# Moving a router's choice into the middle of a block product, and the next adjacency one gap later, in a fused graph-attention and expert kernel

## The chip, the cores and the metric

The kernel runs on one core of one Trainium2 chip. A core has five engines that matter here, each with an instruction queue of its own: TensorE (PE in the profile, its weight loads PEld), VectorE (DVE), ScalarE (ACT), GpSimd (POOL) and SyncE (SP), which only starts transfers. They meet through semaphores. The metric is the device time of one execution in microseconds (us), as the median of several runs.

## The reference

There are 128 graphs of 128 nodes with 1024 features, and a 0/1 adjacency for each graph. First a graph attention with 16 heads of 64 features is added, then a mixture of two out of eight low-rank experts. Cut to what matters:

```python
def gnn(h, adj, W, a):                       # h = layernorm(x)
    Wh = h @ W                               # 128 x 1024 for each graph
    e = leaky_relu(Wh1 + Wh2)                # both per node and head: Wh . a
    att = softmax(where(adj == 0, NEG_INF, e), axis=-1) * adj
    return elu(att @ Wh)

x = x + gnn(layernorm(x), adj, W, a)

y = layernorm(x)
logits = y[:, 0, :] @ router_w.T             # first node of a graph, 8 experts
gates = softmax(top-2 of logits, the rest -inf)
x = x + y + sum over the two experts e: gate_e * (y @ down_e.T) @ up_e.T     # rank 16
```

## The kernel before

The graphs are taken in pairs, q = 0 to 63, and for the experts in groups of four, g = 0 to 31. For one pair `project` multiplies the 256 rows by W in a scheme of seven block products (a Strassen-Winograd form) in place of eight. Each product is eight matmuls of 260 columns in float32; the trace has two matmul records for each. The products of a pair accumulate in three PSUM tiles, "x", "y" and "z", that share a pool of two buffers, taken in turn:

```python
ps_w = ctx.enter_context(tc.tile_pool(name="ps_w", bufs=2, space=bass.MemoryType.PSUM))
# ...
def product(dst, first, lhs, rhs, half_way=None):
    order = [(j, k) for j in range(2) for k in range(KH)]     # KH = 4
    # ... (another order for q == 0)
    for at, (j, k) in enumerate(order):
        if half_way and at == KH:
            half_way()
        nc.tensor.matmul(dst[:, j, cols], lhs[:, k, :], w_sb[:, rhs, k, j, cols],
                         start=(first and k == 0), stop=(k == KH - 1),
                         skip_group_check=not first)
# ...
def read(dst, src, plus):
    nc.vector.tensor_tensor(dst[:, :, cols], src[:, :, cols], plus[:, :, cols], ALU.add)
# ... product_1 (x), product_6 (y), product_2 (x), product_5 (y)
def product_7():
    product(*to("z"), s3, T3, None if q else keep("", column_means, "part 1")[0])
    if q:
        read(wh[:, 2], banks["z"], u4)

def product_3():
    product(*to("y"), s4, B22)
    read(wh[:, 0], banks["y"], p1)

def product_4():
    product(*to("z"), a22, NT4, None if q else keep("scores", first_scores)[0])
    read(wh[:, 1], banks["z"], u2)

for step in ((product_1, product_6, product_2, product_5, product_7, product_3, product_4)
             if q else ...):
    step()
    yield
```

Product 3 is the sixth in order. Everything else of the pairs before and after stands in eight gaps, lists of calls that are carried out ahead of the products: what is in `gaps[6]` is issued between product 3 and product 4, `gaps[0]` ahead of product 1. The engines work through their own instructions in the order in which these calls issue them.

```python
for gap in gaps:
    for f, *args in gap:
        f(*args)
    next(products, None)
```

`pair_sums` (gap 4) makes the sums of input blocks for the next pair on GpSimd, four operations on 128x512. `row_parts` (gap 4) multiplies the first rows with the router, and `logits`, `choose` and `fetch` find the two experts of each of the four graphs and fetch their weights from a table in HBM:

```python
def row_parts(g):
    # ... prod = router_sb * row, part = sum of prod, on VectorE
    nc.vector.tensor_tensor(st["add"][:, 0:G * E].rearrange("p (g e) -> p g e", g=G),
                            of_graph[:, :, None].to_broadcast([P, G, E]),
                            part[:, None].to_broadcast([P, G, E]), ALU.mult)

def logits(g):
    st["pl"] = ps_m.tile([P, HALF], F32, tag="pm", name="pl")
    nc.tensor.matmul(st["pl"][:, 0:G * E + G], ones, st["add"], start=True, stop=True)

def choose(g):
    nc.vector.tensor_copy(lg, st["pl"][:, 0:G * E]...)
    for s in range(TOP):                                # TOP = 2
        if s:
            nc.vector.tensor_tensor(mark, by_order, val[:, 0, :, 0:1]..., ALU.is_equal)
            nc.vector.scalar_tensor_tensor(lg, mark, NO_ENTRY, lg, op0=ALU.mult, op1=ALU.add)
        nc.vector.tensor_reduce(top[:, s], lg, AX.X, ALU.max)
        nc.vector.tensor_tensor(mark, lg, top[:, s, :, None]..., ALU.is_equal)
        nc.vector.tensor_tensor(mark, mark, by_order, ALU.mult)
        nc.vector.tensor_reduce(val[:, 0, :, s], mark, AX.X, ALU.max)
    nc.vector.tensor_tensor(pr[:, 0], top[:, 1], top[:, 0], ALU.subtract)
    nc.vector.tensor_tensor(pr[:, 0], pr[:, 0], st["dev"], ALU.mult)

def fetch(g):
    # ... four small operations on VectorE make the row numbers at_down and at_up
    for j in range(G * TOP):
        nc.gpsimd.indirect_dma_start(out=st["down"]..., in_=table, in_offset=...at_down[:, j:j + 1])
    nc.gpsimd.indirect_dma_start(out=st["up"], in_=up_t, in_offset=...at_up[:, 0:1])
```

`group_adj` counts the entries of each row of the four adjacencies and makes the value that a masked entry is given; `load_adj` loads the adjacencies of the next group, into `adj_i` (one buffer, SyncE's queue) and `adj_f` (two buffers, GpSimd's queue). The attention of a group first uses `n` and `neg` in gap 0 of the following pair.

```python
def group_adj(g):
    nc.vector.tensor_scalar(nz, st["adj_i"], 0.0, None, op0=ALU.not_equal)
    nc.vector.tensor_reduce(n[:, 0], nz, AX.X, ALU.add)
    nc.gpsimd.tensor_scalar(n[:, 1], n[:, 0], -1.0, float(N), op0=ALU.mult, op1=ALU.add)
    nc.gpsimd.tensor_scalar(full, n[:, 1], 0.0, NO_ENTRY, op0=ALU.is_equal, op1=ALU.mult)
    nc.gpsimd.tensor_scalar(neg, full, NEG_INF, None, op0=ALU.min)
```

`high` (ScalarE, gaps 6 and 7) and `low` (VectorE) split a block of the result into two parts for the attention's matmuls, `attend` (gaps 1 and 2). `ffn_down` and `ffn_up` apply the fetched experts during the odd pair that follows.

Of the kernel before, what the change touches and what calls it, by code (L numbers as in the profile page):

```python
# [14 lines left out]
ALU = mybir.AluOpType  # L15
AX = mybir.AxisListType

NEG_INF = -9000000000000000.0
NO_ENTRY = -3.0e38
# [6 lines left out]
def adj_ffn_kernel(  # L26
# [16 lines left out]
    nc = tc.nc  # L43
    B, N, D = x.shape
# [14 lines left out]
    NG, _, G, _ = adj.shape  # L59
# [28 lines left out]
    B11, B21, B22, T1, T2, T3, NT4 = range(7)  # L88
# [317 lines left out]
    def group_adj(g):  # L406

        st = GRP[g]
        nz = work.tile([P, G, N], F32, tag="hp", name="nz")
        nc.vector.tensor_scalar(nz, st["adj_i"], 0.0, None, op0=ALU.not_equal)  # L410

        n = small.tile([P, 2, G], F32, tag="n", name="n")
        nc.vector.tensor_reduce(n[:, 0], nz, AX.X, ALU.add)
        nc.gpsimd.tensor_scalar(n[:, 1], n[:, 0], -1.0, float(N), op0=ALU.mult, op1=ALU.add)

        full = small.tile([P, G], F32, tag="full", name="full")
        nc.gpsimd.tensor_scalar(full, n[:, 1], 0.0, NO_ENTRY, op0=ALU.is_equal, op1=ALU.mult)
        neg = small.tile([P, G], F32, tag="negv", name="negv")
        nc.gpsimd.tensor_scalar(neg, full, NEG_INF, None, op0=ALU.min)
        st.update(n=n, neg=neg)  # L420

    def project(q):

        xt = XT.pop(q)
        a11, a12, a22 = xt[:, 0, 0:KH], xt[:, 0, KH:KC], xt[:, 1, KH:KC]
        s1, s2, s3, s4 = SUMS.pop(q)

        wh = WH[q] = work.tile([P, 3, 2, QE], F32, tag="wh", name="wh", bufs=1)
        if q:
            SC[q] = small.tile([P, 2, HPQ], F32, tag="sc", name="sc")
        PARTS[q] = work.tile([P, 2, 2 * NH, HALF], F32R, tag="parts", name="parts", bufs=1)


        cols = slice(0, QE) if q else MAIN

        def bank():
            return ps_w.tile([P, 2, HALF], F32, tag="pw", name="pw")  # L440

        def product(dst, first, lhs, rhs, half_way=None):
            order = [(j, k) for j in range(2) for k in range(KH)]
            if q == 0:
                order.sort(key=lambda at: at[1])
# [7 lines that stand above are left out]
        def temp(tag):  # L453
            return work.tile([P, 2, QE], F32, tag=tag, name=tag, bufs=1)

        def read(dst, src, plus):
            nc.vector.tensor_tensor(dst[:, :, cols], src[:, :, cols], plus[:, :, cols], ALU.add)  # L457

        p1, u2, u4 = (temp(n) for n in ("p1", "u2", "u4"))
        WH["p1"] = p1  # L460
        banks = {}

        def to(name):
            if name not in banks:
                banks[name] = bank()
                return banks[name], True
            return banks[name], False

        def product_1():
            product(*to("x"), a11, B11)  # L470
            nc.scalar.copy(p1[:, :, cols], banks["x"][:, :, cols])

        def product_2():
            product(*to("x"), a12, B21, None if q else keep("", column_means, "part 0")[0])
            WH[q, 0] = banks["x"]
            if q:
                high(q, 0)
                nc.scalar.copy(SC[q], banks["x"][:, :, SCORES])

        def product_6():  # L480
            product(*to("y"), s2, T2)
            read(u2, banks["y"], p1)

        def product_5():
            product(*to("y"), s1, T1)
            read(u4, banks["y"], p1)
            if q == 0:
# [5 lines that stand above are left out]
                read(wh[:, 2], banks["z"], u4)  # L493

        def product_3():
            product(*to("y"), s4, B22)
            read(wh[:, 0], banks["y"], p1)

        def product_4():
# [5 lines that stand above are left out]
                     if q else  # L505
                     (product_1, product_2, product_7, product_6, product_5, product_3, product_4)):
            step()
            yield
# [7 lines left out]
    def high(q, b):  # L516
        block, rstd = of_block(q, b)
        nc.scalar.mul(in_two(PARTS[q][:, 0, b]), block, rstd)  # L518
# [383 lines left out]
    def correct(less, halves):  # L902
        c, by = (WH[0, 0], less[:, 2:3]) if halves == 2 else (WH["p1"][:, :, MAIN], less[:, 0:1])
        nc.vector.scalar_tensor_tensor(c, w_mean[0], by, c, op0=ALU.mult, op1=ALU.add)

    got = {}

    def keep(name, f, *of):

        def task():  # L910
            got[name] = f(*(got.get(o, o) for o in of))
        return (task,)
# [23 lines left out]
    for q in range(NQ + 2):  # L936
        gaps = [[] for _ in range(8)]
        if q == 0:
            prepare(gaps)
        g, part = divmod(q - 2, 2)  # L940
        ffn = 0 <= g < NG
        if ffn and not part:
            gaps[6] += [(logits, g), (choose, g)]
            if g < NG - 1:
                gaps[6].append((fetch, g))
        if q < NQ:
            gaps[6] += [(high, q, 3), (high, q, 1)]
            gaps[7].append((high, q, 2))
# [49 lines left out]
            gaps[5].insert(0, (ffn_up, (g, 0)))  # L998
            gaps[6].append((ffn_up, (g, 1)))
        if q % 2 == 0 and q < NQ:  # L1000
            gaps[5].append((group_adj, q // 2))
            if q // 2 + 1 < NG:
                gaps[5].append((load_adj, q // 2 + 1))
        if q < NQ:
            if q:
                gaps[3].insert(0, (low, q, 0))
# [62 lines left out]
```

## Time and profile before

| what | value |
|---|---|
| median of 3 runs | 1895.14 us (1893.79 to 1895.28) |
| span of the profiled execution | 1893.3 us |
| TensorE busy | 1880.4 us, 99% |
| VectorE busy | 1714.6 us, 91% |
| ScalarE busy | 1085.0 us, 57% |
| GpSimd busy | 836.6 us, 44% |
| granted TensorE clock | 0.999 |

Busy time is the sum of an engine's executions, and a wait is the time in which it had none, put down to what released it. In a timeline line the first number is the start in us, the second the duration, then engine, line of the kernel, operation, tiles written and read, and in brackets the idle time ahead. Line 449 is the block products, 457 `read`, 727 the router's matmul, 694 the end of `row_parts`, 740 to 757 `choose`, 787 to 790 `fetch` on VectorE, 794 its transfers, 399 to 403 the pair sums, 410 and 413 `group_adj`, 522 `low`, 518 `high`.

### The profile page before, as it was taken

The numbers are of one execution on the slowest core, as the hardware profiler recorded it, in microseconds if no ns is written. First come the engines' busy times: TensorE is split into PE (matmuls) and PEld (weight loads), VectorE is DVE, ScalarE is ACT, GpSimd is POOL, SyncE is SP. The second block draws the span as 40 slices with busy tenths as digits, with TensorE's granted clock in tenths as the row PEclk, the third lists the DMA queues.
The fourth block names the chain that finished last, engine by engine and source line by source line (L and its number), as shares of the span: only waits on it lengthen the run. The fifth ranks groups of instructions, "written<-read, shape, count | busy, mean of one in ns | idle before, by whom it ended". The sixth has DMA issues, their size and how long they took to land.

```text
span 1893.3 us, 29564 instructions
## 1 busy us (share of the span) xinstructions
PE 1880.4 (99%) x10430; PEld 1553.0 (82%) x10430; DVE 1714.6 (91%) x3643; ACT 1085.0 (57%) x1063; POOL 836.6 (44%) x1173
## 2 busy tenths in 40 slices
PE   9999999999999999999999999999999999999997
PEld 6888888888888888888888888888888888888885
DVE  6899999999999999999999999999999999999997
ACT  3656556556556555565565565565655655655654
POOL 4345443355343355433553433554434544335530
PEclk9999999999999999999999999999999999999999
DMA  8465655655655656556556556565566566565544
GB/s 316 135 194 151 181 179 156 194 183 138 201 177 159 199 155 171 179 158 194 184 135 201 178 160 198 156 168 181 166 189 189 133 194 183 156 195 166 159 154 115
DMA packets 349100, 330.43 MB, mean 175 GB/s; under 512 B 279196, under 2 KB 281372, under 8 KB 348440
## 3 DMA queue, kind: packets, MB, share of 16 engines
q1 hardware_dynamic: 326760, 286.06, 50.6%
q0 software_dynamic: 17008, 40.91, 7.8%
q10 hardware_dynamic: 5184, 1.57, 0.3%
q8 instruction: 83, 1.36, 0.3%
q14 instruction: 65, 0.53, 0.1%
HBM read 194.24 MB, written 68.17 MB: 139 GB/s over the span
## 4 chain that ended last, share of the span: by engine, by line
PE 97%; DVE 2%; issue 1%; POOL 0%; DMA 0%; DVEq 0%; ACT 0%
PE pw L449 82%; PE ph L566 6%; PE pu L824 4%; PE pd L808 3%; POOL down L794 0%; PE pu L884 0%; PE idle L160 0%; DVE stats L346 0%; DMA down<-table,at_down 0%; PE pl L727 0%; DVE parts L522 0%; PE rows L238 0%; PE pd_all L859 0%; PE pc L209 0%; DVE xn L828 0%
## 5 line engine op out<-in xcount | busy, mean ns | idle before, releaser
L449 PE MATMUL pw<-w_sb,xt 128*128 128x260 f32 (+1 forms) x4080 | 936.3, 385 | 0.1
L449 PEld LDWEIGHTS pw<-w_sb,xt 128*128 128x128 f32 x4080 | 767.7, 190 | 146.0 <-issue 30.9
L449 PE MATMUL pw<-w_sb,s 128*128 128x260 f32 (+1 forms) x3072 | 707.9, 383 | 0.0
L449 PEld LDWEIGHTS pw<-w_sb,s 128*128 128x128 f32 x3072 | 580.7, 190 | 115.2 <-issue 12.6
L350 POOL TENSOR_SCALAR rstd<-mv 128x2 f32<-128x2 f32 x126 | 27.3, 217 | 847.4 <-DVE mv L347 842.1
L641 ACT COPY y_t<-tt 128x2048 uint16<-128x2048 uint16 x126 | 316.2, 2509 | 111.9 <-DMA tt<-halves 111.6
L635 ACT COPY halves<-xn 128x2048 uint16<-128x2048 uint16 x126 | 239.3, 1899 | 144.4 <-DVE xn L586 101.3
L346 DVE BATCH_NORM_STATS2 stats<-xn 128x6 f32<-128x512 f32 x500 | 316.3, 674 | 0.0
L794 POOL DMA_INDIRECT down<-table,at_down x248 | 259.3, 1045 | 91.1 <-issue 65.2
L583 ACT ACTIVATE ex<-hp 128x1024 f32<-128x1024 f32 x128 | 135.4, 1058 | 229.6 <-DVE hp L576 173.0
L518 ACT ACTIVATE parts<-wh,rstd 128x512 fp32r<-128x512 f32 x192 | 130.9, 714 | 197.7 <-DVE wh L457 197.7
L828 DVE SCALAR_TENSOR_TENSOR xn<-pu,rstd,xn 128x512 f32<-128x512 f32 x248 | 169.1, 745 | 19.9 <-PE pu L824 19.5
L576 DVE TENSOR_TENSOR hp<-ph,att 128x512 f32<-128x512 f32 x256 | 161.2, 671 | 10.1 <-PE ph L566 9.8
L586 DVE SCALAR_TENSOR_TENSOR xn<-ex,xn 128x1024 f32<-128x1024 f32 x126 | 154.4, 1225 | 13.6 <-issue 0.5
L566 PE MATMUL ph<-parts,adj_f 128*128 128x512 f32 x512 | 164.8, 443 | 1.3 <-ACT parts L518 0.8
L584 DVE SCALAR_TENSOR_TENSOR xn<-hp,xn 128x1024 f32<-128x1024 f32 x128 | 156.8, 1225 | 4.4
L661 ACT ACTIVATE xn<-xn,off,mul 128x1024 f32<-128x1024 f32 x128 | 151.3, 1231 | 0.0
L522 DVE SCALAR_TENSOR_TENSOR parts<-wh,rstd,parts 128x512 fp32r<-128x512 f32 x192 | 137.7, 745 | 1.6 <-ACT parts L518 1.5
L566 PEld LDWEIGHTS ph<-parts,adj_f 128*128 128x128 f32 x512 | 96.6, 189 | 21.1 <-ACT parts L518 1.2
L457 DVE TENSOR_TENSOR wh<-pw,u 128x520 f32<-128x520 f32 (+1 forms) x128 | 88.0, 688 | 10.7 <-PE pw L449 10.4
L351 POOL TENSOR_TENSOR rstd<-rstd,half_pow 128x2 f32<-128x2 f32 x126 | 90.2, 716 | 10.5
L457 DVE TENSOR_TENSOR u<-pw,p 128x520 f32<-128x520 f32 (+1 forms) x128 | 86.0, 672 | 6.9 <-remote 3.9
(175 smaller groups left out, 1456.4 us busy)
## 6 DMA issues: line engine op xcount, KB each, us to landing
xn<-in_x SPq DMA_DIRECT2D x128, 512.0 KB
xt<-in_x_t SPq DMA_DIRECT2D x127, 512.0 KB
out_y<-xn SPq DMA_DIRECT2D x124, 512.0 KB
adj_f<-in_adj_t POOLq DMA_DIRECT2D x32, 256.0 KB
adj_i<-in_adj SPq DMA_DIRECT2D x32, 256.0 KB
down<-table,at_down POOLq DMA_INDIRECT x248
w_sb<-in_w SPq DMA_DIRECT2D x3, 1040.0 KB
wt_sb<-in_w_t SPq DMA_DIRECT2D x1, 2048.0 KB
```

The lines of the kernel that those rows point to most:

```text
L346: nc.vector.bn_stats(st[:, h, :], X[i][:, h * HALF:(h + 1) * HALF])
L449: nc.tensor.matmul(dst[:, j, cols], lhs[:, k, :], w_sb[:, rhs, k, j, cols], start=(first and k == 0), stop=(k == KH - 1), skip_group_check ...
L457: nc.vector.tensor_tensor(dst[:, :, cols], src[:, :, cols], plus[:, :, cols], ALU.add)
L566: nc.tensor.matmul(PH[i][h], GRP[g]["adj_f"][:, t, :], PARTS[q][:, s, NH * (i % 2) + h], start=(s == 0), stop=(s == 1))
L576: nc.vector.tensor_tensor(hp[:, h * HALF:(h + 1) * HALF].rearrange("p (h f) -> p h f", f=F), ph.rearrange("p (h f) -> p h f", f=F), att[:, ...
L584: nc.vector.scalar_tensor_tensor(xt, hp, 0.0, xt, op0=ALU.max, op1=ALU.add)
L586: nc.vector.scalar_tensor_tensor(xt, ex, 1.0, xt, op0=ALU.min, op1=ALU.add)
L635: nc.scalar.copy(halves, X[i].bitcast(U16).rearrange("p (d s) -> p s d", s=2))
L641: nc.scalar.copy(y_of(i).bitcast(U16).rearrange("p k (n s) -> p s k n", s=2), TT.pop(i).rearrange("p (s k) n -> p s k n", s=2))
L661: nc.scalar.activation(X[i], X[i], AF.Identity, bias=GRP[g]["off"][:, t:t + 1], scale=GRP[g]["mul"][:, t:t + 1])
L794: nc.gpsimd.indirect_dma_start(out=st["down"][:, j * R:(j + 1) * R].rearrange("p r k -> p (r k)"), out_offset=None, in_=table, in_offset=b ...
L828: nc.vector.scalar_tensor_tensor(y[:, cols], pu[t], st["rstd"][:, t:t + 1], y[:, cols], op0=ALU.mult, op1=ALU.add)
```

## The change

For all groups but the last, logits, choice and fetch are no longer called in gap 6 of the even pair, behind product 3, but from within product 3, after four of its eight matmuls. On VectorE the choice so comes ahead of the `read` of product 3. Reading the adjacency and loading the next one move from gap 5 to gap 6, and the three small operations of `group_adj` move from GpSimd to VectorE, so that they do not stand in GpSimd's queue behind the nine transfers of the fetch. The fetch is meant to start earlier.

```diff
-        nc.gpsimd.tensor_scalar(n[:, 1], n[:, 0], -1.0, float(N), op0=ALU.mult, op1=ALU.add)
+        nc.vector.tensor_scalar(n[:, 1], n[:, 0], -1.0, float(N), op0=ALU.mult, op1=ALU.add)
...
-        nc.gpsimd.tensor_scalar(full, n[:, 1], 0.0, NO_ENTRY, op0=ALU.is_equal, op1=ALU.mult)
+        nc.vector.tensor_scalar(full, n[:, 1], 0.0, NO_ENTRY, op0=ALU.is_equal, op1=ALU.mult)
...
-        nc.gpsimd.tensor_scalar(neg, full, NEG_INF, None, op0=ALU.min)
+        nc.vector.tensor_scalar(neg, full, NEG_INF, None, op0=ALU.min)
...
         def product_3():
-            product(*to("y"), s4, B22)
+            product(*to("y"), s4, B22, between.get(q))
             read(wh[:, 0], banks["y"], p1)
...
+    between = {}
...
         if ffn and not part:
-            gaps[6] += [(logits, g), (choose, g)]
-            if g < NG - 1:
-                gaps[6].append((fetch, g))
+            if g == NG - 1:
+                gaps[6] += [(logits, g), (choose, g)]
+            else:
+                between[q] = lambda g=g: [f(g) for f in (logits, choose, fetch)]
...
         if q % 2 == 0 and q < NQ:
-            gaps[5].append((group_adj, q // 2))
+            gaps[6].append((group_adj, q // 2))
             if q // 2 + 1 < NG:
-                gaps[5].append((load_adj, q // 2 + 1))
+                gaps[6].append((load_adj, q // 2 + 1))
```

## The prediction

> **What bounds the kernel now.** I read the page first, then the waits of TensorE, then the timeline of one period. From the page, the busy row and the chain's shares by engine:
>
> ```profile
> PE 1880.4 (99%) x10430; PEld 1553.0 (82%) x10430; DVE 1714.6 (91%) x3643; ACT 1085.0 (57%) x1063; POOL 836.6 (44%) x1173
> PE 97%; DVE 2%; issue 1%; POOL 0%; DMA 0%; DVEq 0%; ACT 0%
> ```
>
> TensorE is busy for 99% of the span and carries 97% of the chain that ended last. Busy time of TensorE is modelled, so I checked it against starts. In the timeline below, the 16 matmul records of the sixth product begin at 668.52 and the router's matmul at 672.02: 3.50 us for 16, 0.219 us each, and that spacing holds through the products. The waits of TensorE hold only a handful of entries below 2.5 us each; away from the start and the end there is one in the whole run:
>
> ```profile
> PE pt L650 <- DVE xn L589: 2.4, 1, 2.4
> ...
> PE pd L808 <- DMA down<-table,at_down: 0.5, 1, 0.5
> ```
>
> The second, at 750 us, delays the next products by 0.95 us in all (58.64 us from one group's logits to the next, against 57.69 in all others). That one event is all that a better fetch can win. So in the steady part, 31 groups of 57.69 us, there is hardly anything to remove, and the question is whether the change brings in a wait.
>
> Here is the stretch the change touches, from the timeline at 668 to 677 us (start, duration, engine, line, operation):
>
> ```profile
> 668.52 3.67 PE L449 MATMUL pw<-w_sb,s 128*128 128x260 f32 x16
> ...
> 668.80 1.34 POOL L400 TENSOR_TENSOR s<-s,xt 128x512 f32<-128x512 f32 x1
> ...
> 669.49 0.69 DVE L694 TENSOR_TENSOR add<-of_graph,part 128x32 f32<-128x32 f32 x1
> 670.10 1.29 POOL L402 TENSOR_TENSOR xt<-xt 128x512 f32<-128x512 f32 x1
> 670.11 0.69 DVE L457 TENSOR_TENSOR wh<-pw,u 128x520 f32<-128x520 f32 x1
> 670.72 0.95 DVE L410 TENSOR_SCALAR nz<-adj_i 128x512 f32<-128x512 int32 x1
> 671.34 1.47 POOL L403 TENSOR_TENSOR s<-xt,s 128x512 f32<-128x512 f32 x1
> ...
> 672.02 0.31 PE L727 MATMUL pl<-add,ones 128*128 128x36 f32 x2
> ...
> 672.30 0.69 DVE L457 TENSOR_TENSOR wh<-pw,p 128x520 f32<-128x520 f32 x1
> ...
> 672.91 0.18 DVE L740 COPY lg<-pl 128x32 f32<-128x32 f32 x1
> ...
> 673.35 0.19 DVE L752 TENSOR_TENSOR mark<-lg,top 128x32 f32<-128x32 f32 x1
> 673.57 0.19 DVE L753 TENSOR_TENSOR mark<-mark,order 128x32 f32<-128x32 f32 x1
> ...
> 676.36 0.21 DVE L790 TENSOR_SCALAR at_up<-of_slot,up_row 128x1 uint32<-128x1 f32 x1
> ```
>
> VectorE works without a pause here, in the order of the program. The reader should see two things: the second read of `wh` (672.30, block product 3) is what frees the PSUM bank of that product, and today it stands ahead of the choice; and the four pair sums of GpSimd end at 672.81, just before the choice begins.
>
> **What the Trainium skill says.** (1) "SBUF — State Buffer", section "Who interferes with whom": a VectorE instruction with two inputs in SBUF contends with a GpSimd instruction that reads SBUF, and the one that comes second is blocked until the first is through. The trace agrees. L694 writes 128x32 in 0.69 us, while L753 with the same output size takes 0.19 us: L694 began inside GpSimd's L400 (to 670.14) and ended at 670.18, directly behind it. The start of the run shows both directions:
>
> ```profile
> 38.67 1.27 POOL L402 TENSOR_TENSOR xt<-xt 128x512 f32<-128x512 f32 x1
> ...
> 38.93 1.56 DVE L522 SCALAR_TENSOR_TENSOR parts<-c,rstd,parts 128x512 fp32r<-128x512 f32 x1
> ...
> 39.90 1.73 POOL L403 TENSOR_TENSOR s<-xt,s 128x512 f32<-128x512 f32 x1
> ```
>
> L522 elsewhere takes 0.745 us and here 1.56: it waits for L402 to end (39.94), works to 40.49, and then L403 ends 1.14 us later at 41.63. So a waiting instruction gets its turn at the hand-over, and GpSimd's sum then holds the port for about 1.14 us. (2) "PSUM — Partial Sum Buffer", section "Engine vs sequencer instructions": the queue of VectorE is strictly first in, first out; the order in the timeline is the program's. So whatever the choice waits for, the read of `wh` behind it waits too. (3) "TensorE: Matmul & The Clock Gate", section "Step-by-step: what each phase is for": weight loads are pulled ahead of running matmuls, matmuls stay in order. In the trace a weight load takes 190 ns inside the 219 ns of a matmul, ahead of its own. After an interruption that head start is gone: from the first matmul after the router's (672.16) to the second it is 0.303 us, by the starts in the trace, instead of 0.219.
>
> **The change part by part.** All times below count from the start of the sixth product (668.52 = 0). The period and what comes before it are not touched, because VectorE's lag there is set by earlier waits.
>
> Logits half-way: 8 x 0.219 = 1.75. Their input `add` (L694) ends at 670.18, or 1.66. A hand-over from VectorE to TensorE takes about 0.1 us (at the start of the run the weights combined at 19.07 release a weight load at 19.18). So they start at about 1.77 to 1.80: a wait of some 0.05 us a group, new. The two matmuls cost the same as before.
>
> Choice: at the end of the run the copy of the logits starts 0.41 us after their first matmul (1876.03 to 1876.44, VectorE idle). Half-way that is 2.21; the read of `wh` for product 7 (670.11) hands over after about 0.6 us, at 2.2. So L740 starts at about 2.25, instead of 4.39 (672.91). L752 would start 0.44 later, at 2.69, and L753 0.66 later, at 2.91. Now the pair sums are in the way. L402 runs to 671.39 (2.87) and holds the port to about 2.75, so L752 is held only a little. But L403 then takes the port at about 2.9 and keeps it 1.14 us, to about 4.04. L753 reads `mark` and `order`, both in SBUF, and asks at 2.91: it is blocked to 4.04 and ends at 4.2 instead of 3.1. **The choice is lengthened by 1.1 us.** The later operations meet only the two-element operations of L350 and L351, which do not hold the choice up today either (673.19 to 673.91 beside L752 and L753 at 0.19 us).
>
> Read of product 3: choice and fetch now stand ahead of it. From L740 to what follows L790 is 672.91 to 676.49 = 3.58 us. So the read starts at 2.25 + 3.58 + 1.1 = 6.93 and ends at 7.62, instead of 4.47 (672.30 + 0.69). It frees the bank that is called `y` in this pair. With two buffers and the names x, y, z taken in turn, the next pair's `x` falls on exactly that bank. Product 4 follows at 3.64 and takes 3.50, so the next pair's first product is due at 7.14. It may start at 7.62 + 0.1 = 7.72: **a wait of 0.58 us**, and 0.08 us more for the lost head start of the weights (0.303 - 0.219): 0.66 us.
>
> Adjacency, one gap later: its two large operations leave the pair sums' neighbourhood (L410 begins there under L402 and ends 0.3 us after it: 0.95 us, of which I put some 0.5 down to the port; 0.45 us alone is an estimate) and come after the read. Three operations of GpSimd go to VectorE, about 0.22 us each from start to start as in the choice: +0.66 us. From 7.6: L410 to 8.0, L413 (672.30 - 671.70 = 0.6 to the next) to 8.65, three small ones to 9.3, two `low` (0.70 each) to 10.7, the read of product 4 to 11.4. The bank this last read frees is needed by product 6 of the next pair, at 11.69 today and 12.35 with the wait: hidden. Attention's matmuls, 10.53 today and 11.2 then, need a `low` that is done at 10.7: hidden. VectorE then runs some 1.3 us later than today against 0.66 for TensorE, and meets its pauses of 0.2, 0.35 and 1.0 us in the odd pair (697 to 703 us), which take up the rest.
>
> Fetch: its first DMA can start at about 6.8 instead of 7.83 (676.35), and the load of `adj_f` no longer stands ahead. TensorE waits for the fetched rows once in the run, so the gain is at most 0.95 us in all.
>
> Sum: 31 groups (the last keeps its place) x (0.66 + 0.05) = 22.0 us, less 0.95: 21 us. 1895.1 + 21 = **1916 us**, 1.1% more.
>
> **Rivals.** (a) No blocking of L753, because VectorE keeps the port or the sums shift: the read of product 3 ends at 6.5, 0.6 us ahead of need, and nothing but the 0.05 us of the logits is left. 1893.5 to 1897 us. For it: the distance is small, and the choice is placed as if to fit the gap. Against it: L694 and L522 above, both of the same kind. (b) L403 wins the port ahead of L752: 0.23 us more, 0.9 us a group, 1924 us. (c) VectorE becomes the bound: it is 91% busy and gets 31 x 0.66 = 20 us more, but pauses of about 2 us a period are left, so 57.69 us still hold it. Against, unless L410 and the descriptor work of the fetch, now side by side, block each other by up to 1 us; then the read of product 4 is late as well, and 1930 us and more is possible. (d) The earlier fetch pays: against, one wait of 0.95 us in the whole run.
>
> **Range and chances.** I give the blocked case with its variants about 70%, (a) about 22%, (c) the rest. The range of 1894 to 1927 covers (a) nearly whole up to 1.0 us a group (31 x 1.0 = 31). Two per cent is 37.9 us, 1.2 us a group, which takes two blockings: 5%. Faster by 2% would need 38 us that TensorE does not wait for: 1%.
>
> **What would show it.** In the changed profile: L753 with a mean well above 0.19 us (half of its 64 executions near 1.3); a wait of a weight load for VectorE's `wh` L457, 31 times, about 0.6 us each; 58.4 us between groups; no wait at `pd` for the table's DMA; L410 at about 0.45 us. If L753 stays at 0.19, rival (a) holds and my step of the port is wrong. If TensorE waits for the same L457 but at product 6, my order of VectorE's work is.

## The result, and the profile after

The changed kernel takes 1909.96 us (1909.16 to 1910.41, 6 runs), the kernel before 1895.04 us in the same comparison: a ratio of 1.0079, 95% interval 1.0066 to 1.0092. It is 14.9 us slower. The prediction was 1916 us, with a range of 1894 to 1927.

First the page of the changed kernel: the busy row, and the shares of the chain that ended last.

```profile
PE 1891.7 (99%) x10430; PEld 1547.3 (81%) x10430; DVE 1751.5 (92%) x3739; ACT 1082.0 (57%) x1063; POOL 798.8 (42%) x1077
...
PE 66%; DVE 29%; issue 3%; ACT 1%; DMA 1%; DVEq 0%; SPq 0%; ACTq 0%
```

TensorE is still busy for 99% of the span, but the chain now runs through VectorE for 29% of it, where it was 2%. That is a sign that TensorE has begun to wait for VectorE at regular points. The router's matmuls of two successive groups now start 58.16 us apart (the usual distance in the trace), where it was 57.69: 0.47 us a group, and over the 30 distances between the 31 groups that makes 14.1 us of the 14.9.

One period of the changed kernel, from its timeline. Product 3 begins at 498.92, so subtract that to compare with the times counted from product 3 in the prediction.

```profile
498.92 1.92 PE L449 MATMUL pw<-w_sb,s 128*128 128x260 f32 x8
...
499.91 0.69 DVE L694 TENSOR_TENSOR add<-of_graph,part 128x32 f32<-128x32 f32 x1
...
500.74 0.38 PE L727 MATMUL pl<-add,ones 128*128 128x36 f32 x2
...
501.16 0.19 DVE L740 COPY lg<-pl 128x32 f32<-128x32 f32 x1
...
501.61 0.23 DVE L752 TENSOR_TENSOR mark<-lg,top 128x32 f32<-128x32 f32 x1
501.75 1.28 POOL L403 TENSOR_TENSOR s<-xt,s 128x512 f32<-128x512 f32 x1
501.88 1.20 DVE L753 TENSOR_TENSOR mark<-mark,order 128x32 f32<-128x32 f32 x1
...
505.65 1.13 POOL L794 DMA_INDIRECT down<-table,at_down  x1 [1.52 <-DVE of_slot L765]
...
505.79 0.69 DVE L457 TENSOR_TENSOR wh<-pw,p 128x520 f32<-128x520 f32 x1
...
506.53 3.37 PEld L449 LDWEIGHTS pw<-w_sb,xt 128*128 128x128 f32 x16 [0.47 <-DVE wh L457]
```

Two things are to be seen. L753, which took 0.19 us before, takes 1.20 us and ends at 503.08, just after the pair sum L403 (503.03). And the read of product 3, behind it in VectorE's queue, ends at 506.48: 0.05 us later the weight load of the next pair's first product starts, which had been waiting for that read. By the starts in the trace this product begins 0.23 us late in most groups, and its second matmul follows after 0.323 instead of 0.219 us, as its weights were not loaded ahead. Together 0.33 us. The remaining 0.14 us is at the logits. Set against the kernel before, matmul for matmul, TensorE falls back at these two places of the period and nowhere else. The profile's list of waits of the weight loads has both (it counts the idle time of the weight loads, which is more than the delay of the products):

```profile
PEld pw L449 <- DVE wh L457: 14.0, 29, 0.8
...
PEld pl L727 <- POOL s L400: 9.6, 30, 1.3
```

The second line names GpSimd's pair sum, though the logits don't read it. They read `add`, made by VectorE's L694, which ended 0.05 us after that sum because it had been held by it; a release is put down to an engine by nearness in time, so this name is to be taken with care. The run with the logits' input in PSUM, below, settles it.

### The profile page after: what moved, and what is told of

Its sections match the earlier page's. It is cut to its first block, busy times and chain, and to the rows that moved or that the text cites. A ratio compares the mean times of both kernels' runs of the same rounds, so it can differ in the third digit from the quotient of the medians.

```text
span 1908.3 us, 29532 instructions
## 1 busy us (share of the span) xinstructions
PE 1891.7 (99%) x10430; PEld 1547.3 (81%) x10430; DVE 1751.5 (92%) x3739; ACT 1082.0 (57%) x1063; POOL 798.8 (42%) x1077
## 4 chain that ended last, share of the span: by engine, by line
PE 66%; DVE 29%; issue 3%; ACT 1%; DMA 1%; DVEq 0%; SPq 0%; ACTq 0%
PE pw L449 54%; DVE stats L346 8%; PE ph L566 5%; PE pu L824 3%; PE pd L808 3%; DVE xn L584 2%; DVE mark L753 2%; DVE hp L576 2%; DVE u L457 2%; DVE wh L457 2%; DVE parts L522 1%; DVE xn L586 1%; DVE add L694 1%; DVE mv L347 1%; DVE prod L690 1%
## 5 line engine op out<-in xcount | busy, mean ns | idle before, releaser
L449 PE MATMUL pw<-w_sb,s 128*128 128x260 f32 (+1 forms) x3072 | 715.5, 384 | 0.0
L794 POOL DMA_INDIRECT down<-table,at_down x248 | 241.0, 972 | 113.4 <-issue 59.4
L522 DVE SCALAR_TENSOR_TENSOR parts<-wh,rstd,parts 128x512 fp32r<-128x512 f32 x192 | 137.8, 746 | 1.8 <-ACT parts L518 1.8
```

The costliest lines, as they stand in the source:

```text
L522: nc.vector.scalar_tensor_tensor(in_two(PARTS[q][:, 1, b]), block, rstd, in_two(PARTS[q][:, 0, b].bitcast(F32)), op0=ALU.mult, op1=ALU.sub ...
L794: nc.gpsimd.indirect_dma_start(out=st["down"][:, j * R:(j + 1) * R].rearrange("p r k -> p (r k)"), out_offset=None, in_=table, in_offset=b ...
```

## The experiments

The theory (P in the expectations): the fourth pair sum of GpSimd holds the SBUF port that it shares with VectorE (the prediction's first point) and blocks the choice for 1 us; the read of product 3, behind the choice, frees its bank late; the logits have a wait of their own. The rivals: the move of the adjacency costs (A), or the choice ahead of the read costs by its own length, port or not (O).

### The logits alone half-way

```diff
-                between[q] = lambda g=g: [f(g) for f in (logits, choose, fetch)]
+                between[q] = lambda g=g: logits(g)
+                gaps[6] += [(choose, g), (fetch, g)]
```

The adjacency stands as before the change here.

> Only the logits stand half-way; choice, fetch and adjacency are where they were before. This measures the wait of the logits for their input by itself. Theory P: 0.155 us a group as in the changed kernel (1.82 instead of 1.75 us from the start of product 3, and 0.084 us for the next matmul), 31 times 4.8 us: 1899 to 1900 us. A theory in which the logits are free: 1895 us.

Measured: 1899.69 us, ratio 1.0024 (1.0017 to 1.0032); the groups are 57.83 us apart. So the logits cost 0.14 us a group by themselves, 4 to 5 us of the 15. The expectation had the place right and the parts not: half of the 0.14 is their later start, the other half the router's own two matmuls, which take 0.38 us in place of 0.31. The 0.084 us of the matmul behind them is no new cost, since it is there before the change too (0.303 us from its start to the next in both kernels).

### The choice half-way, the adjacency left where it was

In `group_adj` the three small operations are back on GpSimd, and both calls are back in gap 5:

```diff
-            gaps[6].append((group_adj, q // 2))
+            gaps[5].append((group_adj, q // 2))
...
-                gaps[6].append((load_adj, q // 2 + 1))
+                gaps[5].append((load_adj, q // 2 + 1))
```

> The choice half-way, the adjacency left in gap 5 and its three small operations on GpSimd, as before. Theory P (port): the choice is slow in the changed kernel because its second marking (L753) asks for the port just after the fourth pair sum took it. Here L410 and L413 stand ahead of the choice, so the choice begins after most of that sum and L753 stays near 0.2 us; but the read of product 3 stands behind 1.6 us more of VectorE's work and ends at 8.1 us from the start of product 3 (7.56 in the changed kernel), so the next pair's first product waits about 0.9 us a group and the time is about 1926 us. Theory A (the move of the adjacency is what costs): that cost is gone, about 1898 to 1900 us.

Measured: 1925.86 us, ratio 1.0159 (1.0142 to 1.0176), groups 58.71 us apart, all executions of L753 between 191 and 194 ns. The timeline shows why it is slow all the same:

```profile
506.26 0.38 PE L727 MATMUL pl<-add,ones 128*128 128x36 f32 x2
...
506.64 0.96 DVE L410 TENSOR_SCALAR nz<-adj_i 128x512 f32<-128x512 int32 x1
...
508.24 0.18 DVE L740 COPY lg<-pl 128x32 f32<-128x32 f32 x1
...
511.85 0.69 DVE L457 TENSOR_TENSOR wh<-pw,p 128x520 f32<-128x520 f32 x1
...
512.60 3.77 PE L449 MATMUL pw<-w_sb,xt 128*128 128x260 f32 x16 [0.61 <-DVE wh L457]
```

The copy of the logits could have begun at about 506.67 (an estimate: 0.41 us behind their first matmul, as the prediction read it), but L410 and L413 come first, and the choice starts 1.6 us later. The next pair's first product waits for the read ending at 512.54. Theory A falls: without the move of the adjacency the half-way choice costs twice as much (31.0 us instead of 14.9). The move makes room for the choice.

### The adjacency alone

The kernel before with the other half of the diff: `group_adj` and `load_adj` in gap 6, the small operations on VectorE.

> The adjacency a gap later with its small operations on VectorE, the choice in its old place behind the read of product 3. Theory P: no wait of the first product, L753 at 0.19 us; but L410 to L419 (1.9 us) now stand ahead of both low and of the read of product 4, which ends at about 11.9 instead of 10.0; product 6 of the next pair needs that bank at 11.5 to 11.7, so a wait of about 0.4 us a group shows there: about 1907 us. Theory A: the whole 15 us or nearly, 1908 to 1911 us, with the wait at the next pair's first product. If the adjacency is free: 1895 us.

Measured: 1902.59 us, ratio 1.0040 (1.0026 to 1.0054), 58.00 us apart in most groups: 0.31 us each.

```profile
508.19 0.69 DVE L457 TENSOR_TENSOR wh<-pw,u 128x520 f32<-128x520 f32 x1
...
509.00 3.15 PEld L449 LDWEIGHTS pw<-w_sb,s 128*128 128x128 f32 x15 [0.26 <-issue]
```

A wait was expected at the second product of the next pair (its input is `s`), behind the read of product 4. Little of it is there: the read ends at 508.88, in time for the product's start, and only its second matmul is late, 0.09 us in all. The other 0.21 us are at product 7 of that pair. Its PSUM bank comes free when `low` (L522) has read it, and that ends 21.88 us after the logits, where it was 20.38 before. The list of waits of the weight loads names it once a group:

```profile
PEld pw L449 <- DVE parts L522: 11.6, 31, 0.4
```

So the size was nearly right (0.4 expected, 0.3 measured) and the place mostly wrong. L410 took 0.41 us away from the pair sums, against 0.95 beside them. Neither half of the change is free alone, and the parts don't add up: 7.7 us and 31.0 us alone, 14.9 together. Each half shifts VectorE's work ahead of a different read of a bank.

### The fourth pair sum out of the way

The changed kernel, with the fourth operation of `pair_sums` as a call of its own in gap 6, behind the fetch in GpSimd's queue:

```diff
-        nc.gpsimd.tensor_tensor(s4, a12, s2, ALU.subtract)
         SUMS[q] = (s1, s2, s3, s4)
+        if q < 2:
+            last_sum(q, xt)
+    def last_sum(q, xt=None):
+        ...
+        nc.gpsimd.tensor_tensor(s4, xt[:, 0, KH:KC], s2, ALU.subtract)
...
+                gaps[6].append((last_sum, q + 1))
```

> The changed kernel with the fourth pair sum (s4) issued in gap 6, on GpSimd behind the fetch, so that it isn't beside the choice. Theory P: L753 at about 0.2 us in all executions, the read of product 3 ends about 1.0 us earlier, at 6.55, and the wait of the next pair's first product is gone; what stays is the logits' 0.155 us a group: 1899 to 1900 us. Theory O (the choice ahead of the read costs by its own length, port or not): 1908 to 1911 us.

Measured: 1901.02 us, ratio 1.0028 (1.0017 to 1.0039), groups 57.83 us apart but for one (59.21). L753, here line 759, by its source in the profile:

```profile
L759 DVE TENSOR_TENSOR mark<-mark,order x64: 191/192/194, 97.9 to 1886.5; 128x32 f32<-128x32 f32 x64
```

The wait at the first product is gone with the block, the choice still ahead of the read: theory O falls. It is 1 us above what was expected, about what the one long group adds.

### The same instructions with one input in SBUF

Moving GpSimd's sum could help in more than one way. This run leaves GpSimd as it is. The marks of the choice and the first entry found are kept in free columns of the logits' PSUM tile:

```diff
-        mark = small.tile(shape, F32, tag="mark", name="mark", bufs=2)
+        mark = st["pl"][:, 64:64 + G * E].rearrange("p (g e) -> p g e", g=G)
+        first = st["pl"][:, 96:96 + G]
...
-                                        val[:, 0, :, 0:1].to_broadcast(shape), ALU.is_equal)
+                                        first[:, :, None].to_broadcast(shape), ALU.is_equal)
...
-            nc.vector.tensor_reduce(val[:, 0, :, s], mark, AX.X, ALU.max)
+            nc.vector.tensor_reduce(val[:, 0, :, s] if s else first, mark, AX.X, ALU.max)
+        nc.vector.tensor_copy(val[:, 0, :, 0], first)
```

> The changed kernel with the marks of the choice, and the first entry found, kept in free columns of the logits' PSUM tile, so that the second marking (L754 here, L753 before) and the two operations after it have at most one input in SBUF; one small copy is added (0.2 us). The four pair sums of GpSimd stay where they are. Theory P in the form that two SBUF inputs are what is blocked: no execution of that marking near 1.2 us, the read of product 3 ends at about 6.6 to 6.9 us from the start of product 3 instead of 7.56, no wait of the next pair's first product: 57.83 us from group to group and 1899 to 1901 us. A theory in which any small VectorE operation beside a pair sum is blocked, or in which the order alone costs: 1908 to 1911 us.

Measured: 1898.23 us, ratio 1.0020 (1.0012 to 1.0029), groups 57.83 us apart but for one (58.18). From its timeline, the same place:

```profile
500.04 1.28 POOL L403 TENSOR_TENSOR s<-xt,s 128x512 f32<-128x512 f32 x1
500.19 0.20 DVE L754 TENSOR_TENSOR pl<-pl,order 128x32 f32<-128x32 f32 x1
```

The same multiplication, inside the same pair sum, takes 0.20 us once one of its inputs, and here its output too, is in PSUM. The next run tells the two apart. So it is the second SBUF input that is blocked, as the Trainium skill has it in "SBUF — State Buffer", section "Who interferes with whom": with at most one SBUF input, and outside the modes that use both ports, VectorE doesn't contend with GpSimd. L410 has one SBUF input and still took 0.95 us beside the pair sums; whether it ran in such a mode, no run here shows.

### The logits' input as well

On top of that, the sums of `row_parts` go to the PSUM tile, so that L694 has one input in SBUF:

```diff
-        part = small.tile([P, E], F32, tag="part", name="part", bufs=1)
+        st["pl"] = ps_m.tile([P, HALF], F32, tag="pm", name="pl")
+        part = st["pl"][:, 128:128 + E]
...
-        st["pl"] = ps_m.tile([P, HALF], F32, tag="pm", name="pl")
+        if g == NG - 1:
+            st["pl"] = ps_m.tile([P, HALF], F32, tag="pm", name="pl")
```

> The run with the marks in PSUM, with one thing more: the sums of row_parts (its second operation) are also written to the logits' PSUM tile, so that the operation that makes the logits' input (L694 before, 128x32) has one input in SBUF instead of two. All four pair sums and the half-way logits stay where they are. Theory P: that operation takes about 0.2 us instead of 0.69, the logits' input is ready about 0.5 us earlier, their wait (0.14 us a group) goes too, and the groups are 57.69 us apart: 1893.5 to 1896 us, against 1898.2 with the marks alone. If the logits wait for something else than this blocked operation: 1898 us.

Measured: 1893.64 us, ratio to the kernel before 0.9993 (0.9984 to 1.0001), groups 57.69 us apart. The operation that was L694, in the profile of that tile, first in the changed kernel and then here (shortest, median and longest in ns):

```profile
L694 DVE TENSOR_TENSOR add<-of_graph,part x31: 686/692/697, 93.4 to 1839.4; 128x32 f32<-128x32 f32 x31
```

```profile
L695 DVE TENSOR_TENSOR add<-of_graph,pl x31: 186/186/188, 93.2 to 1823.6; 128x32 f32<-128x32 f32 x31
```

Here the output, `add`, is in SBUF as before, and only one input has moved. The same trace has the opposite case, an operation with both inputs in SBUF and its output in PSUM (L755), next to the multiplication with one:

```profile
497.27 1.28 POOL L402 TENSOR_TENSOR xt<-xt 128x512 f32<-128x512 f32 x1
...
498.22 0.39 DVE L755 TENSOR_TENSOR pl<-lg,top 128x32 f32<-128x32 f32 x1
498.51 1.27 POOL L403 TENSOR_TENSOR s<-xt,s 128x512 f32<-128x512 f32 x1
498.64 0.20 DVE L756 TENSOR_TENSOR pl<-pl,order 128x32 f32<-128x32 f32 x1
```

L755 is held until L402 ends (498.55) and is done 0.06 us later; L756 runs inside L403 unhindered. So it is the inputs that count, not the output. Both waits of the change were the same port. With the changed order kept whole and the small tiles moved to PSUM, the 14.9 us are gone. Against the kernel before, the interval of the ratio holds 1. The trace shows what the earlier fetch is worth: the wait for the fetched rows is gone, no group is longer than 57.77 us, and the 30 distances sum to 1730.87 us instead of 1731.74, 0.9 us less, the gain that the prediction had put at 0.95 at most.

### The logits after five matmuls instead of four

```diff
-                if half_way and at == KH:
+                if half_way and at == (KH + 1 if q else KH):
```

> The changed kernel with the logits after five of the eight matmuls of product 3 instead of four. Their input is ready by then, so their own wait (0.14 us a group) goes. Theory P: the choice is held by the fourth pair sum to the same moment (about 4.0 us from the start of product 3), so the read of product 3 ends at 7.5 as before, while the next pair's first product is due 0.14 us earlier and waits that much longer. The two waits don't add up: 58.15 to 58.2 us from group to group, 1909 to 1911 us. If the waits were independent: 1905 to 1906 us. If the choice were simply pushed 0.44 us later: 1915 us and more.

Measured: 1916.10 us, ratio 1.0113 (1.0097 to 1.0128), groups 58.39 us apart. This missed. The logits' wait is gone, but the choice was not held to the same moment:

```profile
503.22 1.27 POOL L403 TENSOR_TENSOR s<-xt,s 128x512 f32<-128x512 f32 x1
503.37 1.17 DVE L752 TENSOR_TENSOR mark<-lg,top 128x32 f32<-128x32 f32 x1
...
504.57 0.19 DVE L753 TENSOR_TENSOR mark<-mark,order 128x32 f32<-128x32 f32 x1
```

The choice begins 0.30 us later, so VectorE finds the port taken one operation earlier: L752 is blocked, and L753 follows only after the sum. The read of product 3 ends 0.21 us later (7.77 us from the start of product 3 instead of 7.56), and the next product is due 0.15 us earlier. Its delay grows by 0.36 us, the logits' wait of 0.14 is saved, and the group is 0.23 us longer (the parts are rounded). This is the order of the prediction's rival (b), which had put the later read at 0.23 us. The time lies in what was expected of a choice "simply pushed", but that isn't what happened: the later start and the block at L752 together move the read by half of 0.44 us.

### Both mended in time

The changed kernel with the fourth sum in gap 6 and the logits after five matmuls.

> The changed kernel with the fourth pair sum in gap 6 behind the fetch and the logits after five of eight matmuls: both waits should go. Theory P: 57.69 us from group to group as before the change, no wait for the fetched rows, 1893.5 to 1896 us, so no better than the kernel before by more than 1 us. If more is hidden in the change: 1898 us or above.

Measured: 1894.62 us, ratio 1.0001 (0.9992 to 1.0009), 57.69 us apart in most groups. One group is 58.68. With both waits gone the change costs nothing, and it brings nothing that this measurement shows.

### The three small operations left on GpSimd

The changed kernel with `n`, `full` and `neg` on GpSimd as before.

> The changed kernel with the three small operations of group_adj left on GpSimd. They then stand in GpSimd's queue behind the nine transfers of the fetch (some 11.5 us), and the attention's mask value comes about 6 us after VectorE asks for it. VectorE has about 2 us of pauses in a period to take that up, so TensorE should wait some 4 to 5 us a group: 2020 to 2080 us. If the mask value isn't waited for: 1905 to 1910 us.

Measured in a single execution: 2116.54 us, 64.86 us from group to group, with a mean granted TensorE clock of 0.952.

```profile
500.98 0.19 DVE L543 TENSOR_TENSOR m<-e,negv 128x32 f32<-128x32 f32 x1 [7.53 <-POOL negv L419]
...
502.22 1.65 PE L566 MATMUL ph<-parts,adj_f 128*128 128x512 f32 x3 [3.99 <-DVE parts L522]
503.67 5.46 PE L449 MATMUL pw<-w_sb,xt 128*128 128x260 f32 x16
...
508.96 3.67 PE L449 MATMUL pw<-w_sb,s 128*128 128x260 f32 x16
```

VectorE waits 7.5 us for the mask value, behind the fetch's transfers in GpSimd's queue. The attention's matmuls need a `low` that stands behind the mask in VectorE's queue, and TensorE stands still 4.0 us for it, about as expected. But a group is 7.2 us longer than before the change. 0.47 us of that is what the changed kernel loses anyway, 4.2 us is lost up to the end of the standstill, and 2.5 us more behind it, most of it in the product that follows: its 16 matmul records take 5.46 us where a later product takes 3.67. The granted clock was 0.50 from 502.2 to 507.3 and 1.00 from 509.0 to 512.5. So the expected wait was right, and what was missed is that after this standstill TensorE ran at half its clock for a while. With the fetch ahead of them in GpSimd's queue, these three operations have to be on VectorE.

## Why the prediction was right, and where its sum was off

**No gain to be had.** Right. The wait for the fetched rows is gone, and the first transfer starts 6.73 us after product 3 began (505.65), expected 6.8, before 7.83. It brought nothing that can be seen: in place of the one long group of the kernel before (58.64) the changed kernel has three, two of 58.52 and 58.51 us, in which VectorE starts L787 0.35 us later than in the others, and one of 59.53 us, in which L690 met a pair sum and the logits waited 1.3 us. This last group is a natural control:

```profile
1139.80 1.50 DVE L690 TENSOR_TENSOR prod<-router_sb,first_row 128x256 f32<-128x256 f32 x1 [0.22 <-issue]
...
1142.41 1.26 POOL L403 TENSOR_TENSOR s<-xt,s 128x512 f32<-128x512 f32 x1
...
1143.76 0.19 DVE L753 TENSOR_TENSOR mark<-mark,order 128x32 f32<-128x32 f32 x1
```

L753 came only after L403 there (which ends at 1143.67), and took 0.19 us. Ahead of L690 VectorE stood idle for 0.22 us, for which the profile names nothing that it waited for; why, stays open, and so does the late L787.

**The block of L753.** Right, in place and size: expected from 2.91 to 4.2 after the start of product 3, measured from 2.96 to 4.16.

**The read of product 3.** Right: expected from 6.93 to 7.62, measured from 6.87 to 7.56.

**The wait of the next pair's first product.** Right in kind, too large: 0.66 expected (0.58 and 0.08 for the late weights), 0.33 measured (0.23 and 0.10). The failed step is the one that set when that product is due. I took 7.14: product 4 starting at 3.64 as before, and 3.50 for it. It is due at 7.39. First, the late weights behind the router's matmuls, 0.08 us, which I had read myself (0.303 instead of 0.219), fall into product 4 today and were left out: the product starts at 7.23 in the kernel before (675.75). Second, the logits' own new cost of about 0.15 us stands ahead of it. The rest, some 0.1 us, is that the read ends 0.06 us earlier than expected and that the hand-over takes 0.05 us, not 0.1. Waits on one engine are not to be added when one moves the deadline of the next.

**The logits.** 0.05 us expected, 0.14 measured. They started at 1.82, near the 1.77 to 1.80 expected and 0.07 late. But I wrote that the two matmuls cost the same as before. They don't: their first weight load had to wait too, so it wasn't done ahead, and the pair takes 0.38 us instead of 0.31.

**The sum.** 0.71 us a group was expected, 0.47 measured: 21 us against 14.9. The two terms erred in opposite directions (0.33 too much, 0.09 too little), so the sum is nearer than its larger term, and that much is luck. Both mis-sized terms are about weights loaded ahead and about who moves whose deadline, not about the port.

**Hidden parts.** Right: no wait at product 6 and none at attention's matmuls in the changed kernel. L410 takes 0.59 us, not 0.45; what stands behind it had room for the difference.

## What to carry to other kernels

When an engine's queue is strictly in order, look at what stands behind the thing you move forward: here a bank of PSUM was waiting for the read that the choice overtook. Before putting small VectorE operations beside large GpSimd ones, count their SBUF inputs; one input in PSUM can be worth more than a better place in the order. And in a kernel whose bound engine has no idle time, an earlier transfer is worth only the waits that the trace shows for it.

## What the runs showed of the hardware

A VectorE multiplication of 128x32 with both inputs in SBUF took 1.20 us beside a GpSimd sum of 128x512 and 0.20 us with one input and the output in PSUM; another went from 0.69 to 0.19 us when one input alone moved to PSUM. A choice that starts 0.3 us later changes which of its operations is blocked, and a group grows from 58.16 to 58.39 us. A weight load that wasn't done ahead of its matmul cost 0.07 to 0.10 us in the places measured here. After TensorE had stood still for 4.0 us, the granted clock was 0.50 over the next 5.1 us (three small operations left on GpSimd).
